# Layer 1's small sums on 32x32 tiles of TensorE, with masks stored twice and loaded per step

## The chip, the core and the metric

The kernel runs on one core of one Trainium2 chip. The metric is the device time of one execution in microseconds (us); lower is better. Engines are named as in the profile: PE (TensorE matmuls), PEld (TensorE weight loads), DVE (VectorE), ACT (ScalarE), POOL (GpSimd) and SP (SyncE, which here only issues DMAs).

## What is computed

Two layers on 4096 nodes with 512 features and a dense 4096x4096 matrix `adj`, 1 to 2% of whose elements are not zero. Layer 0 is attention with `adj` added twice to the logits; layer 1 is graph attention with 8 heads of 64 dimensions:

```python
h = relu(layernorm(x));  q, k, v = h @ Wq.T + bq, h @ Wk.T + bk, h @ Wv.T + bv
x = x + softmax(q @ k.T / sqrt(512) + adj + adj) @ v
h = relu(layernorm(x))
nX = standardize((h @ W) per head) * a_ln + b_ln          # 8 heads x 64
kg = leaky_relu(at1[:, :, None] + at2[:, None, :], 0.2) * adj   # at1 = nX.a1, at2 = nX.a2
attention = softmax(where(adj != 0, kg, -32768))
x = x + elu(attention @ nX + nX)
```

## The kernel before

**Layer 0** walks over 256 tiles of 128 sources by 512 targets (`TILES`), two tiles an iteration, with the products of the logits and of the weighted sum regrouped into seven smaller ones. Beside that work `for_layer_1` (L708) makes from each turned tile of `adj` what layer 1 needs: `ng`, bf16, is -2^60 where there is no edge and 0 elsewhere; `gs`, float32, is the edge's weight, and 2^-45 where there is none. Both go to DRAM (`nT_d`, `gT_d`) in DMAs of 128 KB and 256 KB that SP issues.

**Between the layers** the rows are normalized and projected (`turn`, `project`, `standardize`), and `sides` and `fours` put small tensors into DRAM: `z1_d` and `z2_d` hold for each head six bf16 rows (three bf16 parts of a logit's half, and ones), 32 partitions apart, so that a product over 6 rows gives a logit's sum in nearly float32; `u4_d` holds four times the targets' part.

**Layer 1** is a list of 512 steps, `STEPS`: 8 chunks of 512 targets, in each 2 groups of 4 heads (`hg`), in each 32 blocks of 128 sources. A step makes a 128x512 tile of logits for four heads (sources on the partitions, targets along the row). Two of the heads are "left", two "right":

- `left_sums` (L1070), one step ahead: the plain sums of the two left heads into a PSUM tile `l` of two banks. Four matmuls on 64x64 tiles of TensorE; the targets' operand is `z1_left`, a copy of `z1` in which everything but the six rows of the left heads is zero. `left_relu` (L1080): ACT takes four times the positive part, in place.
- `sums` (L1083): four matmuls over 6 rows add all four heads' sums (into `l` for left heads, into the banks `r0`, `r1` for right ones), then eight matmuls on 64x64 tiles add the mask, with the identity as weights. A 64-row tile of TensorE can write either half of the sources from its own 64 rows only, so the mask is held twice in SBUF: `nb`, as it is, and `nx`, with its two halves of 64 rows swapped.
- `right_leaky` (L1105): DVE makes the two right heads' logits, which frees `r0` and `r1`. `right_weigh` (L1117): POOL multiplies them by the edges' weights `g`. `left_weigh` (L1121): DVE does so for the left heads, reading `l`.
- `exponent` (L1124): ACT, two steps later, one instruction for four heads. `values` (L1128): four steps later, four float32 matmuls (eight instructions in the profile) into `accs`, which stays over the 32 steps of a group.
- `finish` (L1177) at a group's end: ACT copies one bank of `accs` and DVE the other, then PE turns the result back to rows, and the group's output is made over the next 21 steps, with three adding DMAs issued by POOL and one store issued by SP. The exponent of that step is cut in two, with the copies in between.

**Order and loads.** `seq` keeps every instruction of the steps in the order of the program, so each engine and SP's queue work in the order of the loop at L1536. `load_adj` (L1006) runs each fourth step, for the four steps after the next boundary: `z2` (128 KB), `nb` (512 KB, 128 partitions), `nx` (two DMAs of 256 KB, 64 partitions each) and `g` (1 MB, 128 partitions). Each has two buffers. `open_group` (L1033) brings `z1` and the twelve rows of `z1_left` ten steps ahead of a group, `load_u4` the targets' part.

Of the kernel before, what the change touches and what calls it, by code (L numbers as in the profile page):

```python
# [11 lines left out]
BF16 = mybir.dt.bfloat16  # L12
# [6 lines left out]
P = 128  # L19
N = 4096  # L20
D = 512
NH = 8
HD = 64
NB = N // P
SB = 4
# [10 lines left out]
GC = 512  # L36
NI = N // GC
# [42 lines left out]
def fast_path(  # L80
# [18 lines left out]
    nc = tc.nc  # L99
    seq = tc.keep_in_program_order  # L100
# [3 lines left out]
    R = 32  # L104
# [10 lines left out]
    dram = ctx.enter_context(tc.tile_pool(name="dram", bufs=1, space=DRAM))  # L115
# [29 lines left out]
    x1_d = dram.tile([NI, 2, P, SB, 2, P], F32, name="x1_d")  # L145

    gT_d = dram.tile([NB, P, N], F32, name="gT_d")
    nT_d = dram.tile([NB, P, N], BF16, name="nT_d")

# [174 lines left out]
    with tc.tile_pool(name="rows_in", bufs=2) as rows_in, tc.tile_pool(  # L326
# [357 lines left out]
        with tc.tile_pool(name="turns", bufs=6) as turns, tc.tile_pool(  # L684
# [23 lines left out]
            def for_layer_1(s):  # L708
                ic, jt = TILES[s]
                aT = turned[s] if s >= SB else firsts[s]  # L710
                ng = work.tile([P, GC], BF16, name="ng", tag="ng", bufs=2)
                seq(nc.vector.tensor_scalar(ng, aT, 0.0, NEG_BIG, ALU.is_equal, ALU.mult))
                gs = work.tile([P, GC], F32, name="gs", tag="gs", bufs=2)
                seq(nc.vector.scalar_tensor_tensor(gs, ng, G_MASKED / NEG_BIG, aT, ALU.mult, ALU.add))  # L714
                nc.sync.dma_start(out=nT_d[jt, :, ts(ic, GC)], in_=ng)
                nc.sync.dma_start(out=gT_d[jt, :, ts(ic, GC)], in_=gs)

            def product(out, s, name_a, name_b, start):
# [269 lines left out]
    with tc.tile_pool(name="ga_g", bufs=2) as adjs, tc.tile_pool(  # L988
# [5 lines left out]
        JB = 4  # L994
# [4 lines left out]

        later = {}  # L1000

        z1_lefts = [gat.tile([P, GC], BF16, name=f"z1_left{k}") for k in range(2)]
        for z in z1_lefts:
            seq(nc.vector.memset(z, 0.0))

        def load_adj(q):  # L1006
            ic, _, jt = STEPS[q * JB]
            z2 = inputs.tile([P, JB * P], BF16, name="z2", tag="z2", bufs=2)
            seq(nc.sync.dma_start(
                out=z2, in_=z2_d[:, STEPS[q * JB][1], jt * P : (jt + JB) * P]  # L1010
            ))
            ng = inputs.tile([P, JB, GC], BF16, name="nb", tag="nb", bufs=2)
            seq(nc.sync.dma_start(
                out=ng, in_=nT_d[jt : jt + JB, :, ts(ic, GC)].rearrange("t p i -> p t i")
            ))

            nx = inputs.tile([P, JB, GC], BF16, name="nx", tag="nx", bufs=2)
            for r in range(2):
                seq(nc.sync.dma_start(
                    out=nx[ts(r, HD)],  # L1020
                    in_=nT_d[jt : jt + JB, ts(1 - r, HD), ts(ic, GC)].rearrange("t p i -> p t i"),
                ))
            g = adjs.tile([P, JB, GC], F32, name="g", tag="g", bufs=2)
            seq(nc.sync.dma_start(
                out=g, in_=gT_d[jt : jt + JB, :, ts(ic, GC)].rearrange("t p i -> p t i")
            ))
            loads[q] = (g, (ng, nx), z2)

        def cols(ic, hg):
            rows = slice(ic * GC, (ic + 1) * GC)  # L1030
# [2 lines left out]
        def open_group(n, queue):  # L1033

            ic, hg, _ = STEPS[n]
            z1_left = z1_lefts[(2 * ic + hg) % 2]
            for first in (0, HD):
                rows = slice(first, first + 6)
                seq(queue.dma_start(out=z1_left[rows, :], in_=z1_d[rows, hg, ts(ic, GC)]))
            z1 = inputs.tile([P, GC], BF16, name="z1", tag="z1", bufs=2)  # L1040
            seq(queue.dma_start(out=z1, in_=z1_d[:, hg, ts(ic, GC)]))
            u4 = inputs.tile([P, 2, GC], F32, name="u4", tag="u4", bufs=2)
            groups[ic, hg] = {"z1": z1, "z1_left": z1_left, "u4": u4}
            load_u4(n, 0, queue)

        def load_u4(n, e, queue):
# [11 lines left out]

        lefts, rights = {}, {}

        def z_product(n, hh, out, start):

            ic, hg, jt = STEPS[n]
            rows = slice(32 * hh, 32 * hh + 6)
            seq(nc.tensor.matmul(  # L1065
                out, loads[n // JB][2][rows, ts(jt % JB, P)], groups[ic, hg]["z1"][rows, :],
                start=bool(start), stop=False, skip_group_check=not start,
            ))

        def left_sums(n):  # L1070

            lefts[n] = psum.tile([P, 2, GC], F32, name="l", tag="l", bufs=2)
            ic, hg, jt = STEPS[n]
            for r, c in ((0, 0), (1, 1), (0, 1), (1, 0)):
                seq(nc.tensor.matmul(  # L1075
                    lefts[n][ts(c, HD), r, :], loads[n // JB][2][ts(r, HD), jt % JB * P + c * HD :][:, :HD],
                    groups[ic, hg]["z1_left"][ts(r, HD), :], start=True, stop=True,
                ))

        def left_relu(n):  # L1080
            seq(nc.scalar.activation(lefts[n], lefts[n], AF.Relu, scale=4.0))  # L1081

        def sums(n):  # L1083

            jt = STEPS[n][2]
            left = lefts[n]
            right = [psum.tile([P, GC], F32, name=f"r{e}", tag=f"r{e}", bufs=1) for e in range(2)]
            out = [left[:, 0, :], right[0], left[:, 1, :], right[1]]
            for hh in (1, 3, 0, 2):
                z_product(n, hh, out[hh], hh % 2)  # L1090
            masks = loads[n // JB][1]
            for first in (1, 0):
                for r, c in ((0, 0), (1, 1), (0, 1), (1, 0)):
                    rows = ts(r, HD)
                    seq(nc.tensor.matmul(  # L1095
                        out[first + 2 * r][ts(c, HD), :], ident_b[rows, rows],
                        masks[r != c][rows, jt % JB, :], start=False, stop=True,
                        skip_group_check=first == 0,
                    ))
            rights[n] = right  # L1100

        def both_heads(n):
            return loads[n // JB][0][:, STEPS[n][2] % JB, :].unsqueeze(1).to_broadcast([P, 2, GC])

        def right_leaky(n):  # L1105

# [17 lines left out]
        def exponent(n, heads=slice(0, HG)):  # L1124
            t = logits[n][:, heads, :]
            seq(nc.scalar.activation(t, t, AF.Exp))  # L1126
# [337 lines left out]
        def at_block(r, f, *a):  # L1464
            at_blocks.setdefault(r, []).append(lambda: f(*a))
# [26 lines left out]
        at_block(0, rests[0])  # L1492
        at_block(12, first_group)
        at_block(14, load_adj, 0)
        for ic in range(2):
            load_normalized(ic)
        for r in range(-1, NB):
# [38 lines left out]
        for n in range(n_steps + 4):  # L1536

            q = n // JB + 1
            if n == n_steps:

                check_early()
                last_in.append(work.tile([P, HG, GC], F32, name="t", tag="t", bufs=6))
                for k, ap in enumerate((own_d[NI - 1, :, :, 1], x1_d[NI - 1, 1])):
                    seq(nc.sync.dma_start(
                        out=last_in[0][:, 2 * k : 2 * k + 2, :].rearrange("p f c -> p (f c)")
                        .rearrange("p (b d) -> p b d", b=SB),
                        in_=ap.rearrange("p b f d -> p b (f d)"),
                    ))
            if n % JB == 0 and q < n_steps // JB:
                load_adj(q)  # L1550
            if n + 10 < n_steps and STEPS[n + 10][2] == 0:
                open_group(n + 10, nc.sync)
            if n + 6 < n_steps and STEPS[n + 6][2] == 0:
                load_u4(n + 6, 1, nc.sync)
            if n < n_steps:
                sums(n)
            for f in left.pop(n, []):
                f()
            if n + 1 < n_steps:
                left_sums(n + 1)  # L1560
            if n < n_steps:
                right_leaky(n)
                right_weigh(n)
            if n + 1 < n_steps:
                left_relu(n + 1)
            done, ready = 0 <= n - 4 < n_steps, 0 <= n - 2 < n_steps
            if done and n < n_steps + 1:
                values(n - 4, 0)
            extra(n, "mid")
            if n < n_steps:  # L1570
                left_weigh(n)
            if done:
                if n < n_steps + 1:
                    values(n - 4, 1)
                if n % JB == 3:
                    loads.pop((n - 4) // JB)
            if n == n_steps + 3:
                for m, hf in ((n - 6, 0), (n - 5, 0), (n - 6, 1), (n - 5, 1)):
                    values(m, hf)
                for hf in range(2):  # L1580
                    values(n - 4, hf)
            if done and STEPS[n - 4][2] == NB - 1:
                if ready:
                    exponent(n - 2, slice(0, 2))
                finish(n, *STEPS[n - 4][:2])
                if ready:
                    exponent(n - 2, slice(2, 4))
            elif ready:
                exponent(n - 2)
            extra(n, "end")  # L1590
# [404 lines left out]
```

## Time and profile before

| | |
|---|---|
| time, median of 3 runs (3539.04 to 3541.75) | 3539.05 us |
| the profiled execution: its time, its span | 3538.39 us, 3536.6 us |
| PE busy | 3492.0 us (99%) |
| DVE busy | 2574.3 us (73%) |
| POOL busy | 2285.6 us (65%) |
| ACT busy | 1771.1 us (50%) |
| moved by DMA | 779.07 MB, 220 GB/s on average |

All times are of one execution seen by the hardware profiler. "Span" is from the first to the last instruction. A share of busy time is a mean over stages: layer 0 with its projections takes about the first 1775 us, layer 1's steps run from about 1935 to 3514 us. "DMA share" is the time that the packets on the core's 16 DMA engines took, as a share of 16 engines' time; packets can overlap, so a stretch can read above 1. Matmul durations overlap too, since matmuls are pipelined: what a matmul occupies is read from the distance between starts, or from the chain of waits, which gives each piece only the time by which it moved the end. A group name such as "L1095 PE MATMUL r<-nb,ident_b 64*64 64x512" has the line, the engine, the operation, output and inputs, the array's rows and columns in use, and the moving operand's shape.

### The profile page before, as it was taken

Reading aid. Unit: us, or ns where it says so; the run is one execution under the profiler, and the core shown is the slowest. Engines: PE = TensorE matmul, PEld = TensorE weight load, DVE = VectorE, ACT = ScalarE, POOL = GpSimd, SP = SyncE. Lnnn points to the kernel's source line nnn. Section 1 sums busy time; section 2 is a strip of 40 time slices with the busy share of each in tenths; the row PEclk is TensorE's granted clock in tenths of the full one; section 3 lists DMA queues with packets and bytes.
Section 4 is the critical chain, followed back from the end, with each engine's and each line's share of the span. In section 5 each row is a group of like instructions: output and inputs, shape, how many; then the busy total and the mean of one; then the engine's idle time right before and its main releaser. Section 6 shows DMA issues by size and latency. Waiting matters only on the chain.

```text
span 3536.6 us, 59808 instructions
## 1 busy us (share of the span) xinstructions
PE 3492.0 (99%) x21898; PEld 2149.6 (61%) x21898; DVE 2574.3 (73%) x4262; ACT 1771.1 (50%) x1580; POOL 2285.6 (65%) x1863
## 2 busy tenths in 40 slices
PE   9999999999999999999999999999999999999998
PEld 7888888888888888888887223223222323232232
DVE  6765665656565666656567888888888888888887
ACT  2100111111111111111133999999999999999997
POOL 6754444444444444444567888788888888888886
PEclk9999999999999999999999999999999999999999
DMA  6688888888888888888768777787778877777885
GB/s 226 219 247 246 233 232 250 234 244 247 235 246 247 231 252 241 237 248 232 235 135 183 210 207 204 205 208 214 211 209 219 214 215 206 198 209 209 214 213 147
DMA packets 633550, 779.07 MB, mean 220 GB/s; under 512 B 78560, under 2 KB 461216, under 8 KB 624032
## 3 DMA queue, kind: packets, MB, share of 16 engines
q1 hardware_dynamic: 615680, 742.34, 73.5%
q0 software_dynamic: 16464, 31.98, 5.3%
q8 instruction: 174, 2.85, 0.3%
q10 hardware_dynamic: 1104, 0.85, 0.1%
q14 instruction: 128, 1.05, 0.1%
HBM read 592.97 MB, written 174.19 MB: 217 GB/s over the span
## 4 chain that ended last, share of the span: by engine, by line
PE 90%; DVE 7%; ACT 1%; DMA 1%; issue 1%; SPq 0%; DVEq 0%; ACTq 0%
PE accs L1134 25%; PE XZ L722 21%; PE M L777 20%; PE r L1095 4%; PE r L1065 4%; PE l L1075 3%; PE X L508 3%; PE l L1095 3%; PE Z L508 2%; DVE t L1122 2%; PE y L1327 1%; PE pt L1198 1%; DVE x L837 1%; DVE y L1211 1%; PE accs L1327 1%
## 5 line engine op out<-in xcount | busy, mean ns | idle before, releaser
L1119 POOL TENSOR_TENSOR t<-t,g 128x1024 f32<-128x1024 f32 x512 | 1225.6, 2406 | 268.9 <-DVE t L1113 233.3
L1134 PE MATMUL accs<-t,nX 128*64 128x512 f32 x4096 | 1003.0, 605 | 4.6 <-DVE ob L1188 4.6
L1126 ACT ACTIVATE t<-t 128x2048 f32<-128x2048 f32 (+1 forms) x527 | 976.5, 1853 | 0.2 <-POOL t L1119 0.2
L1113 DVE SCALAR_TENSOR_TENSOR t<-u,at2m,r 128x512 f32<-128x512 f32 x1024 | 719.3, 744 | 194.2 <-issue 152.0
L738 ACT ACTIVATE aT<-aT 128x512 f32<-128x512 f32 x256 | 161.2, 630 | 1387.3 <-DVE aT L734 1387.3
L734 DVE TENSOR_TENSOR aT<-aT,XZ 128x256 f32<-128x256 f32 x884 | 348.7, 418 | 575.1 <-PE XZ L722 570.8
L1122 DVE TENSOR_TENSOR t<-l,g 128x1024 f32<-128x1024 f32 x512 | 623.4, 1218 | 0.0
L1081 ACT ACTIVATE l<-l 128x1024 f32<-128x1024 f32 x512 | 516.3, 1008 | 117.5 <-PE l L1075 66.2
L1134 PEld LDWEIGHTS accs<-t,nX 128*64 128x64 f32 x4096 | 246.5, 136 | 461.9 <-issue 449.5
L722 PE MATMUL XZ<-qt,hS 128*128 128x256 f32 x2024 | 479.1, 379 | 1.0
L750 POOL TENSOR_TENSOR S<-aT 128x256 f32<-128x256 f32 x128 | 93.5, 731 | 506.9 <-ACT aT L738 506.9
L722 PEld LDWEIGHTS XZ<-qt,hS 128*128 128x128 f32 x2024 | 383.9, 190 | 55.9 <-DVE aT L734 4.0
L722 PE MATMUL XZ<-qt,hT 128*128 128x256 f32 x1520 | 369.5, 379 | 0.0
L762 POOL TENSOR_TENSOR total<-total,aT 128x256 f32<-128x256 f32 x360 | 323.0, 910 | 9.4
L722 PEld LDWEIGHTS XZ<-qt,hT 128*128 128x128 f32 x1520 | 288.8, 190 | 39.3
L1065 PEld LDWEIGHTS <-z 6*128 6x128 bf16 x2048 | 52.4, 91 | 422.2 <-DVE t L1113 353.8
L751 POOL TENSOR_TENSOR aT<-aT 128x256 f32<-128x256 f32 x128 | 93.6, 731 | 284.1 <-ACT aT L738 284.0
L777 PE MATMUL M<-tv,aT 128*128 128x256 f32 x1024 | 262.6, 379 | 0.0
L777 PE MATMUL M<-v,aT 128*128 128x256 f32 x1024 | 262.6, 379 | 0.0
L777 PE MATMUL M<-v,S 128*128 128x256 f32 x1024 | 242.5, 380 | 0.0
L714 DVE SCALAR_TENSOR_TENSOR gs<-ng,aT 128x512 f32<-128x512 bf16 x252 | 222.7, 884 | 8.7
L777 PEld LDWEIGHTS M<-v,aT 128*128 128x128 f32 x1024 | 194.6, 190 | 26.5
(267 smaller groups left out, 4552.4 us busy)
## 6 DMA issues: line engine op xcount, KB each, us to landing
g<-gT_d SPq DMA_DIRECT2D x128, 1024.0 KB
ag<-in_adj_dram SPq DMA_DIRECT2D x256, 256.0 KB
hS<-s_d SPq DMA_DIRECT2D x64, 1024.0 KB
gT_d<-gs SPq DMA_DIRECT2D x256, 256.0 KB
nb<-nT_d SPq DMA_DIRECT2D x128, 512.0 KB
nx<-nT_d SPq DMA_DIRECT2D x256, 256.0 KB
hT<-h_d SPq DMA_DIRECT2D x64, 768.0 KB
tv<-vt_d SPq DMA_DIRECT2D x128, 384.0 KB
```

Source lines behind the costliest of these rows:

```text
L714: seq(nc.vector.scalar_tensor_tensor(gs, ng, G_MASKED / NEG_BIG, aT, ALU.mult, ALU.add))
L722: seq(nc.tensor.matmul(out, a, b, start=start and k == 0, stop=k == 1, skip_group_check=not start,))
L734: seq(nc.vector.tensor_add(p, before, part))
L762: seq(nc.gpsimd.tensor_add(t, t, a))
L777: seq(nc.tensor.matmul(sums[ic][i][:, u, :], a[:, ts(u, P)], b, start=jt == 0 and u == 0, stop=jt == NB - 2, skip_group_check=u == 1,))
L1081: seq(nc.scalar.activation(lefts[n], lefts[n], AF.Relu, scale=4.0))
L1095: seq(nc.tensor.matmul(out[first + 2 * r][ts(c, HD), :], ident_b[rows, rows], masks[r != c][rows, jt % JB, :], start=False, stop=True, ski ...
L1113: seq(nc.vector.scalar_tensor_tensor(t[:, 2 + e, :], u4[:, e, :], at2m[:, jt, h : h + 1], right[e], ALU.max, ALU.add))
L1119: seq(nc.gpsimd.tensor_mul(t[:, 2:4, :], t[:, 2:4, :], both_heads(n)))
L1122: seq(nc.vector.tensor_mul(logits[n][:, 0:2, :], lefts.pop(n), both_heads(n)))
L1126: seq(nc.scalar.activation(t, t, AF.Exp))
L1134: seq(nc.tensor.matmul(accs[ts(e, HD), hf, :], nX[jt // SB][:, jt % SB, hg * HG + 2 * hf + e, :], t[:, hf + 2 * e, :], start=jt == 0, stop ...
```

## The change

It puts layer 1's left sums, its 6-row sums and its mask sums on tiles of 32 rows by 32 columns: head `hh` of the step has rows 32·`hh` to 32·`hh`+31 of TensorE, and each of the four column strips writes one block of 32 sources. A matmul over 128 or 64 columns of weights becomes four or two of 32 columns: 8 matmuls a step for the left sums (before 4), 16 for all heads' sums (before 4), 16 for the masks (before 8). For this each row group needs the whole tile's mask in its own 32 partitions: 32 partitions by 4 blocks by 512 targets, four times. `for_layer_1` stores the mask twice in the new layout; `load_masks` loads a step's masks, 512 KB, in two DMAs of 64 partitions, three steps ahead, into four buffers. `nx`, `z1_left` and their loads go. The load of `g` moves from the first to the second step of each four. At a group's end the copies now come before the whole exponent, which stays one instruction.

```diff
-    nT_d = dram.tile([NB, P, N], BF16, name="nT_d")
+    nT_d = dram.tile([NB, NI, 2, R, SB, GC], BF16, name="nT_d")
...
-                nc.sync.dma_start(out=nT_d[jt, :, ts(ic, GC)], in_=ng)
+                for u in range(2):
+                    nc.sync.dma_start(out=nT_d[jt, ic, u].rearrange("p c i -> c p i"), in_=ng)
                 nc.sync.dma_start(out=gT_d[jt, :, ts(ic, GC)], in_=gs)
...
-        z1_lefts = [gat.tile([P, GC], BF16, name=f"z1_left{k}") for k in range(2)]
-        for z in z1_lefts:
-            seq(nc.vector.memset(z, 0.0))
...
         def load_adj(q):
             ic, _, jt = STEPS[q * JB]
             z2 = inputs.tile([P, JB * P], BF16, name="z2", tag="z2", bufs=2)
             seq(nc.sync.dma_start(
                 out=z2, in_=z2_d[:, STEPS[q * JB][1], jt * P : (jt + JB) * P]
             ))
-            ng = inputs.tile([P, JB, GC], BF16, name="nb", tag="nb", bufs=2)
-            seq(nc.sync.dma_start(
-                out=ng, in_=nT_d[jt : jt + JB, :, ts(ic, GC)].rearrange("t p i -> p t i")
-            ))
-
-            nx = inputs.tile([P, JB, GC], BF16, name="nx", tag="nx", bufs=2)
-            for r in range(2):
-                seq(nc.sync.dma_start(
-                    out=nx[ts(r, HD)],
-                    in_=nT_d[jt : jt + JB, ts(1 - r, HD), ts(ic, GC)].rearrange("t p i -> p t i"),
-                ))
+            loads[q] = {"z2": z2}
+
+        def load_g(q):
+            ic, _, jt = STEPS[q * JB]
             g = adjs.tile([P, JB, GC], F32, name="g", tag="g", bufs=2)
             seq(nc.sync.dma_start(
                 out=g, in_=gT_d[jt : jt + JB, :, ts(ic, GC)].rearrange("t p i -> p t i")
             ))
-            loads[q] = (g, (ng, nx), z2)
+            loads[q]["g"] = g
+
+        masks = {}
+
+        def load_masks(n):
+
+            ic, _, jt = STEPS[n]
+            masks[n] = inputs.tile([P, SB, GC], BF16, name="nb", tag="nb", bufs=4)
+            for r in range(2):
+                seq(nc.sync.dma_start(
+                    out=masks[n][ts(r, HD)], in_=nT_d[jt, ic].rearrange("u p c i -> (u p) c i")
+                ))
...
         def open_group(n, queue):
...
-            z1_left = z1_lefts[(2 * ic + hg) % 2]
-            for first in (0, HD):
-                rows = slice(first, first + 6)
-                seq(queue.dma_start(out=z1_left[rows, :], in_=z1_d[rows, hg, ts(ic, GC)]))
...
-        def z_product(n, hh, out, start):
+        def z_products(n, hh, out, **flags):
 
             ic, hg, jt = STEPS[n]
-            rows = slice(32 * hh, 32 * hh + 6)
-            seq(nc.tensor.matmul(
-                out, loads[n // JB][2][rows, ts(jt % JB, P)], groups[ic, hg]["z1"][rows, :],
-                start=bool(start), stop=False, skip_group_check=not start,
-            ))
+            rows = slice(R * hh, R * hh + 6)
+            for c in range(SB):
+                seq(nc.tensor.matmul(
+                    out[ts(c, R), :], loads[n // JB]["z2"][rows, jt % JB * P + c * R :][:, :R],
+                    groups[ic, hg]["z1"][rows, :], **flags,
+                ))
 
         def left_sums(n):
 
             lefts[n] = psum.tile([P, 2, GC], F32, name="l", tag="l", bufs=2)
-            ic, hg, jt = STEPS[n]
-            for r, c in ((0, 0), (1, 1), (0, 1), (1, 0)):
-                seq(nc.tensor.matmul(
-                    lefts[n][ts(c, HD), r, :], loads[n // JB][2][ts(r, HD), jt % JB * P + c * HD :][:, :HD],
-                    groups[ic, hg]["z1_left"][ts(r, HD), :], start=True, stop=True,
-                ))
+            for r in range(2):
+                z_products(n, 2 * r, lefts[n][:, r, :], start=True, stop=True)
...
         def sums(n):
...
-            for hh in (1, 3, 0, 2):
-                z_product(n, hh, out[hh], hh % 2)
-            masks = loads[n // JB][1]
-            for first in (1, 0):
-                for r, c in ((0, 0), (1, 1), (0, 1), (1, 0)):
-                    rows = ts(r, HD)
+            order = (1, 3, 0, 2)
+            for hh in order:
+                right_one = hh % 2 == 1
+                z_products(n, hh, out[hh], start=right_one, stop=False, skip_group_check=not right_one)
+            for hh in order:
+                rows = ts(hh, R)
+                for c in range(SB):
                     seq(nc.tensor.matmul(
-                        out[first + 2 * r][ts(c, HD), :], ident_b[rows, rows],
-                        masks[r != c][rows, jt % JB, :], start=False, stop=True,
-                        skip_group_check=first == 0,
+                        out[hh][ts(c, R), :], ident_b[rows, rows], masks[n][rows, c, :],
+                        start=False, stop=True, skip_group_check=hh % 2 == 0,
                     ))
+            masks.pop(n)
...
         at_block(14, load_adj, 0)
+        at_block(14, load_g, 0)
+        for n in range(3):
+            at_block(14, load_masks, n)
...
-            if n % JB == 0 and q < n_steps // JB:
-                load_adj(q)
+            if n + 3 < n_steps:
+                load_masks(n + 3)
+            if n % JB < 2 and q < n_steps // JB:
+                (load_adj, load_g)[n % JB](q)
...
             if done and STEPS[n - 4][2] == NB - 1:
-                if ready:
-                    exponent(n - 2, slice(0, 2))
                 finish(n, *STEPS[n - 4][:2])
                 if ready:
-                    exponent(n - 2, slice(2, 4))
+                    exponent(n - 2)
```

## The prediction

> **What bounds the kernel now.** I read the page first, then the chain of waits in a steady stretch of layer 1, the instructions in order of time there, and the busy times of short windows for the DMA engines.
>
> ```profile
> PE 3492.0 (99%) x21898; PEld 2149.6 (61%) x21898; DVE 2574.3 (73%) x4262; ACT 1771.1 (50%) x1580; POOL 2285.6 (65%) x1863
> ...
> ACT  2100111111111111111133999999999999999997
> ...
> DMA  6688888888888888888768777787778877777885
> ```
>
> PE is busy throughout; ACT is idle in layer 0 and nearly full in layer 1, and the DMA engines are three quarters full in both. The change is in layer 1, whose chain repeats with a period of 2.97 us:
>
> ```profile
> 2600.09 1.87 PE accs L1134 x8
> 2601.96 0.32 PE r L1065 x2
> 2602.28 0.01 PE l L1065 x2
> 2602.29 0.34 PE r L1095 x4
> 2602.63 0.22 PE l L1095 x4
> 2602.85 0.22 PE l L1075 x4
> ```
>
> All of it is PE: the values 1.87, the four heads' sums 0.33, the masks 0.34 + 0.22, the left sums 0.22. But the timeline has another engine right behind:
>
> ```profile
> 2602.22 0.14 PEld L1095 LDWEIGHTS <-ident_b 64*64 64x64 bf16 x8 [0.23 <-issue]
> 2602.22 0.40 PE L1095 MATMUL r<-nb,ident_b 64*64 64x512 bf16 x2
> 2602.23 0.40 PE L1095 MATMUL r<-nx,ident_b 64*64 64x512 bf16 x2
> ...
> 2603.11 1.01 ACT L1081 ACTIVATE l<-l 128x1024 f32<-128x1024 f32 x1
> ...
> 2604.03 1.91 ACT L1126 ACTIVATE t<-t 128x2048 f32<-128x2048 f32 x1
> ```
>
> ACT needs 1.01 + 1.90 = 2.91 us a step (its exponent reads 1.90 or 1.91). No PE saving can be worth more than 2.97 - 2.91 = 0.06 us a step. DVE needs 2 x 0.74 + 1.22 = 2.71 and POOL 2.41 by the page's means. That leaves the DMA engines, and here the windows matter (columns: stretch and length, busy times by engine, granted clock, DMA share, GB/s):
>
> ```profile
> 1939.00:3520.00 1581.00, 1564.01 (x12761) 468.29 (x12763) 1343.85 (x1687) 1461.98 (x1072) 1292.14 (x602) 1.00 0.78 208
> ...
> 2628.50:2629.00 0.50, 0.50 (x10) 0.18 (x12) 0.50 (x1) 0.50 (x1) 0.50 (x1) 1.00 1.06 350
> ...
> 2630.50:2632.50 2.00, 2.00 (x22) 0.51 (x18) 1.60 (x3) 2.00 (x2) 1.37 (x1) 1.00 1.02 199
> ...
> 2633.50:2634.50 1.00, 1.00 (x6) 0.14 (x2) 1.00 (x2) 1.00 (x2) 0.49 (x2) 1.00 1.04 393
> ...
> 1779.00:1785.00 6.00, 6.00 (x30) 5.28 (x29) 1.77 (x5) 0.63 (x1) 0.72 (x1) 1.00 1.05 241
> ```
>
> The first is all of layer 1's steps. The next three follow one call of `load_adj`, its DMAs in the order of the queue: `nb` over 128 partitions at 350 GB/s, `nx` in two pieces of 64 partitions at 199, `g` over 128 at 393. `nb` and `nx` have the same 1 KB runs, so the loss is the pieces', not the runs'. The last is between the layers, where SP had twelve loads of `xn_d` queued, each over 32 partitions: 241 GB/s with the engines full. Loads that cover part of the partitions move about half.
>
> **The change part by part.** *TensorE.* The eight mask matmuls, two passes of the array, become sixteen on sixteen different tiles, one pass: the second one's 0.22 us goes. Sums, masks and left sums now have one tile shape; the sums' 0.32 and the first mask pass's 0.34 stand 0.10 to 0.12 above a bare pass of 0.22, a gap at each change of shape, and the one between them goes, about 0.10. So 2.97 - 0.22 - 0.10 = 2.65 us. Added are 24 pairs of weight load and matmul a step. No row shows a 32x32 pair. The eight loads of L1095 take 0.14 us together, 18 ns each: 24 x 18 = 0.43, and a step of 3.08, if none is hidden; four such matmuls start within 0.01 us of each other, some 3 ns apart: 24 x 3 = 0.07, and 2.72. I take 2.72, since the loads overlap matmuls in the trace; both ends stay for the range. The Trainium skill speaks against this part: its page "TensorE: Matmul & The Clock Gate" (section "Wait — 56ns, not 53.3ns?") says that with hardware decoding off the sequencer spends about 62 ns on each matmul. By that, an estimate, 48 matmuls a step would take 2.98 us and nothing would be gained; no row of this trace shows which decoding holds.
>
> *Masks in layer 1.* The bytes double, from 256 to 512 KB a step, and all now come in pieces of 64 partitions, with 4 KB runs. Take a group of 32 steps: 1581 / 16 = 98.8 us, of which the DMA engines are busy 0.78 x 98.8 = 77.1; full stretches read 1.04, so 77.1 / 1.04 = 74.1 us of full work. Out go `nb`, 8 x 524,288 B at 350 GB/s = 12.0, and `nx`, 8 x 524,288 B at 199 = 21.1. What stays (`g`, `z2`, `u4`, the groups' ends) is 41.0 us. In come 32 x 524,288 B. At 393 GB/s, as if halves cost nothing, 42.7; at 199, as `nx`, 84.3; at 241, as the loads of `xn_d`, 69.6 us (2.18 a step). I take 241: there the queue was never empty, as here, and runs were 2 KB, nearer to 4 than `nx`'s 1. The sum is 110.6 us a group, against 98.8 now and 32 x 2.91 = 93.1 of ACT plus the groups' ends: the DMA engines become the bound, at 3.46 us a step. Since they then work without a break, the 98.8 - 32 x 2.97 = 3.8 us that a group's end costs now are inside the 110.6. Cost: 16 x (110.6 - 98.8) = +189 us.
>
> The Trainium skill bears on this row: its page "SBUF — State Buffer" (section "Door 1: The DMA port swizzle (why `[64,N]` ≈ `[32,N]`)") holds that 64 adjoining partitions reach only eight of the sixteen ports, and its section "Can I just issue two DMAs to hit both halves?" that two loads on the two halves gain only 6%. Its 218 GB/s for eight ports, with 6% on top, would be 231 GB/s: by it, an estimate, 72.6 us of masks a group and +237 us.
>
> *The new wait.* The first mask matmul of a step waits for its own load, before for one of four steps ago. Queued behind it on PE are the left sums of the next step and the values; DVE (`right_leaky`), ACT (`left_relu`) and POOL wait for these in turn. On SP, `load_masks` waits until `sums` of the step before has freed its buffer, with `z2`, `g`, `u4` and the output's store behind it; as three steps' masks are then still queued at the engines, they do not run dry. `g` is queued right behind the masks of the step that first uses it and takes 1,048,576 B / 393 GB/s = 2.7 us: POOL and DVE get it late once in four steps, in a gap that the sum already holds. SP itself issues an `nx` piece in 1.39 / 2 = 0.7 us (L1019), so two a step are 1.4 of 3.46 us, with room.
>
> *Layer 0.* 256 more stores of 128 KB. At the 350 GB/s of a 1 KB load that is 0.37 us of DMA each, 256 x 0.37 = 96 us in all, beside PE, whose chain there waited 0.8 us for a DMA in the whole layer; the engines' share goes from 0.83 to about 0.89. On SP each takes 0.32 us and stands ahead of the `gT_d` store and, at times, of `adj` and hidden-state loads; SP waits 824 us there for DVE, so it has the time. I take zero; if the cover is gone, up to 96 us; a gain is excluded, as nothing leaves.
>
> *The rest.* 32 loads of 6 KB and two memsets go: nothing. The copies move ahead of half an exponent, 1.05 us, of which PE waits 0.31 us at a group's end; ACT's copies and halves 2 x 1.05 become one of 1.90. At most 0.5 us x 15, hidden once DMA bounds: zero here.
>
> Sum, on the profiled execution: span 3536.6 + 189 = 3725.6, and 1.8 us outside the span: 3727. The median of the runs stands 0.7 above the profiled one: **3728 us**.
>
> **The rivals.** *ACT becomes the bound (faster).* If the two pieces overlap so that the masks come at over (32 x 524,288 B) / (98.8 - 41.0 us) = 290 GB/s, the DMA work fits into today's period. Then a step is 2.91 us, a group 32 x 0.06 + 0.4 = 2.3 us shorter, the whole 3539 - 37 = 3502 us. For it: shares of 1.05 show packets in flight together, and 4 KB runs pay less per packet. Against it: both rows of partial loads stay at 199 and 241. Chance 0.11.
>
> *The pieces run as `nx` does (slower still).* At 199 GB/s a group is 125.3 us: +26.5 x 16 = +424, 3963 us. PE's pauses could lengthen it: after its stall of 3.56 us at 1941 the granted clock fell (0.91 over 1900 to 2000 us), and mask matmuls took 0.64 instead of 0.40 us. For it: same pieces, same halves; against: `nx` had 1 KB runs and a queue that emptied after it. Chance 0.17 for 3850 and above.
>
> *TensorE doesn't gain and the masks nearly fit.* At 3.08 us a step from unhidden loads, with masks above 290 GB/s, 0.11 x 512 = +56: 3595 us. Chance 0.10 for 3530 to 3640.
>
> **How the numbers follow.** The forecast (DMA bound, 3640 to 3850) has 0.62. The range of 3580 to 3940 leaves out ACT's case (0.11), half of the last rival and the top of the second: about 0.2. Anything within 0.2% (7 us), which is what measurements of this kernel can resolve, needs the masks to hit the break-even closely: 0.02. Faster 0.11, slower 0.87.
>
> **What would show it.** Right: layer 1's DMA share near 1.04 and some 260 GB/s (208 x 98.8 us + 8.4 MB, over 110.6 us); PE waiting at the mask line for a DMA into `nb`; ACT's share of layer 1 down from 92% to about 83%; step distances of 3.46 us on average, uneven by fours; layer 0's slices unchanged; on PE three passes of about 0.22 us in one tile shape. Wrong: DMA share below 0.95 in layer 1, waits for "issue" on PE at the mask or sum lines, a period of 2.91 us with ACT unbroken, or a layer 0 that is longer.

## The result, and the profile after

The changed kernel takes **4118.22 us** (median of 4 runs, 4108.91 to 4134.45), the kernel before 3539.05; the ratio is 1.164, with a 95% interval of 1.162 to 1.166. The direction was forecast, the size was not: 3728 us with a range up to 3940. The profiled execution of the changed kernel took 4121.95 us, its span 4120.1.

The page first, in the rows that were shown of before:

```profile
PE 3643.6 (88%) x34186; PEld 2201.6 (53%) x34186; DVE 2554.1 (62%) x4260; ACT 1767.8 (43%) x1565; POOL 2227.7 (54%) x1863
...
ACT  2100111011111111110237777777777777787776
...
DMA  6677778788788877877689999999999999999997
```

In layer 1 the DMA row stands at 9 nearly from end to end and ACT has gone from 9 to 7: that part of the forecast is there in kind, though ACT was forecast at 83% and, in the window of 2500 to 3400 us below, is at 75%. But ACT's row leaves its low digits, where layer 1 begins, in about the same slice as before, although a slice is now 103 us instead of 88: layer 0 has become longer too. Layer 0 is taken here from the first start of its exponent on ACT (`aT<-aT`) to the last, layer 1 from the first start of a mask matmul to the last:

| us | before | after | difference |
|---|---|---|---|
| layer 0 (256 tiles) | 241.7 to 1785.3 = 1543.6 | 242.3 to 2027.0 = 1784.7 | +241 |
| between the layers | 151 | 154 | +3 |
| layer 1 (16 groups of 32 steps) | 1936.5 to 3511.8 = 1575.3 | 2181.3 to 4095.6 = 1914.3 | +339 |

Layer 1's loss was forecast at 189, layer 0's at zero.

**Layer 1.** The chain of waits over 2600 to 2614 us (start, length, link):

```profile
2599.85 0.27 PE l L1063 x8
2600.12 0.34 SPq L1026
2600.45 0.05 issue
2600.51 15.13 DMA nb<-nT_d
```

Before, this chain was PE from link to link. Now one link, loads of masks behind each other, fills 15 us. The instructions in order of time show the step that the forecast hoped for, and what comes of it:

```profile
2601.87 0.14 PEld L1063 LDWEIGHTS <-z 6*32 6x32 bf16 x16 [0.81 <-DVE t L1107]
...
2604.78 0.41 PE L1063 MATMUL r<-z,z 6*32 6x512 bf16 x8
...
2605.00 0.40 PE L1089 MATMUL r<-nb,ident_b 32*32 32x512 bf16 x8
...
2605.25 0.40 PE L1063 MATMUL l<-z,z 6*32 6x512 bf16 x8
...
2605.58 1.94 PE L1128 MATMUL accs<-t,nX 128*64 128x512 f32 x8
...
2607.45 0.41 PE L1063 MATMUL r<-z,z 6*32 6x512 bf16 x8
...
2612.33 0.61 PE L1089 MATMUL r<-nb,ident_b 32*32 32x512 bf16 x4 [4.45 <-DMA nb<-nT_d]
```

From 2604.78 to 2607.45 runs a whole step with its masks in place: sums 0.22, masks 0.25, left sums 0.33, values 1.87, together 2.67 us. One load of masks later, PE stands for 4.45 us.

**Layer 0.** The list of waits over 150 to 1780 us (engine, tile and line, what it waited for: us in total, times, longest) has two new rows of waits for a DMA, and one of PE's weight loads for POOL; before, PE waited 0.8 us for `tv`, once, and no weight load for POOL:

```profile
PE M L778 <- DMA tv<-vt_d: 120.6, 68, 4.4
...
PEld M L778 <- POOL aT L752: 53.0, 23, 2.6
...
DVE ng L712 <- DMA nT_d<-ng: 50.3, 19, 7.1
```

And yet the DMA engines are *less* busy there than before. The windows (stretch, its length, busy times of PE, PEld, DVE, ACT and POOL, granted clock, DMA share, GB/s), of before:

```profile
300.00:1700.00 1400.00, 1398.28 (x6497) 1228.99 (x6496) 863.06 (x1636) 182.22 (x289) 655.45 (x861) 1.00 0.84 240
```

and of after, with two short ones in which hardly anything but the new stores is under way:

```profile
300.00:1700.00 1400.00, 1263.72 (x5606) 1080.98 (x5607) 722.89 (x1411) 156.34 (x248) 526.22 (x744) 0.97 0.80 227
2500.00:3400.00 900.00, 768.94 (x11644) 231.19 (x11641) 626.38 (x778) 677.17 (x490) 595.26 (x273) 0.92 1.02 242
1006.00:1008.00 2.00, 1.04 (x3) 0.89 (x4) 0.00 (x0) 0.00 (x0) 1.84 (x4) 0.73 0.30 107
1019.00:1022.00 3.00, 3.00 (x16) 2.44 (x15) 1.81 (x3) 0.63 (x1) 0.79 (x2) 1.00 0.26 95
```

A share of 0.26 to 0.30 with a queue of stores waiting is the sign to look for: a quarter of sixteen engines, at 95 GB/s. In these windows, by the reading of the next section, four engines worked and twelve had next to nothing. The packet records of the trace, counted by time, agree: over 1019 to 1022 us four packets were under way for three quarters of the time and never more than seven; over 2603 to 2606 us, in layer 1, never fewer than sixteen. The share is a mean over sixteen, so four full engines look like slack.

### The profile page after: what moved, and what is told of

The parts are those of the page before. It is cut to its first block, busy times and chain, and to the rows that moved or that the text cites. A ratio compares the mean times of both kernels' runs of the same rounds, so it can differ in the third digit from the quotient of the medians.

```text
span 4120.1 us, 85374 instructions
## 1 busy us (share of the span) xinstructions
PE 3643.6 (88%) x34186; PEld 2201.6 (53%) x34186; DVE 2554.1 (62%) x4260; ACT 1767.8 (43%) x1565; POOL 2227.7 (54%) x1863
## 5 line engine op out<-in xcount | busy, mean ns | idle before, releaser
L1128 PE MATMUL accs<-t,nX 128*64 128x512 f32 x4096 | 1110.7, 662 | 7.6 <-DVE ob L1182 7.0
L1120 ACT ACTIVATE t<-t 128x2048 f32<-128x2048 f32 x512 | 973.2, 1901 | 10.9 <-POOL t L1113 10.7
L1128 PEld LDWEIGHTS accs<-t,nX 128*64 128x64 f32 x4096 | 263.1, 145 | 468.9 <-issue 456.2
L1063 PEld LDWEIGHTS <-z 6*32 6x32 bf16 x12288 | 169.6, 89 | 632.9 <-DVE t L1107 292.6
L1063 PE MATMUL l<-z,z 6*32 6x512 bf16 x8192 | 437.7, 403 | 44.6 <-DVE t L1116 23.2
L1089 PE MATMUL r<-nb,ident_b 32*32 32x512 bf16 x4096 | 265.0, 400 | 215.2 <-DMA nb<-nT_d 214.6
L723 PE MATMUL XZ<-qt,hT 128*128 128x256 f32 x1520 | 399.0, 402 | 0.0
L723 PEld LDWEIGHTS XZ<-qt,hT 128*128 128x128 f32 x1520 | 308.1, 203 | 47.6
L778 PE MATMUL M<-tv,S 128*128 128x256 f32 x512 | 167.8, 411 | 155.9 <-DMA tv<-vt_d 140.0
L763 POOL TENSOR_TENSOR total<-total,aT 128x256 f32<-128x256 f32 x360 | 270.5, 765 | 9.4
```

The lines of the kernel that those rows point to most:

```text
L723: seq(nc.tensor.matmul(out, a, b, start=start and k == 0, stop=k == 1, skip_group_check=not start,))
L763: seq(nc.gpsimd.tensor_add(t, t, a))
L778: seq(nc.tensor.matmul(sums[ic][i][:, u, :], a[:, ts(u, P)], b, start=jt == 0 and u == 0, stop=jt == NB - 2, skip_group_check=u == 1,))
L1063: seq(nc.tensor.matmul(out[ts(c, R), :], loads[n // JB]["z2"][rows, jt % JB * P + c * R :][:, :R], groups[ic, hg]["z1"][rows, :], **flags,))
L1089: seq(nc.tensor.matmul(out[hh][ts(c, R), :], ident_b[rows, rows], masks[n][rows, c, :], start=False, stop=True, skip_group_check=hh % 2 == ...
L1128: seq(nc.tensor.matmul(accs[ts(e, HD), hf, :], nX[jt // SB][:, jt % SB, hg * HG + 2 * hf + e, :], t[:, hf + 2 * e, :], start=jt == 0, stop ...
```

## The experiments

Two theories stood at the outset. The first: layer 0 loses because the new store, written in four blocks of 32 rows, runs on four of the sixteen DMA engines; layer 1 loses because loads over 64 partitions are slow. The rival: what costs is the number and the bytes of the new transfers (256 more stores on SP, twice the mask bytes), however they are shaped. The first runs undo the shapes one by one and leave number and bytes as they are. (Letters in the quoted expectations are defined there or name these theories in this order.) Six of the kernels take masks of other sources or of another chunk, as their expectations say, and so do not compute the whole; they serve to time the transfers. Where no number of runs is given, it is one run; the four runs of the changed kernel lie within 26 us.

**The stores as 128 rows.**

```diff
-    nc.sync.dma_start(out=nT_d[jt, ic, u].rearrange("p c i -> c p i"), in_=ng)
+    nc.sync.dma_start(out=nT_d[jt, ic, u].rearrange("p c i -> (p c) i"), in_=ng)
```

> The changed kernel, but both stores of a tile's mask go out as 128 rows of 1 KB in the order of the partitions (destination 128 x 512) and not as 4 blocks of 32 rows (destination 4 x 32 x 512). Same bytes, same number of DMAs; the masks stand in DRAM in another order of sources than the loads take them for, so that each source has another one's mask. Theory A (the stores in four blocks keep only 4 of the 16 DMA engines busy, which the share of 0.26 at 95 GB/s in stretches with nothing else suggests): layer 0, which takes 1785 us from the first to the last exponent in the changed kernel and 1544 before, goes back to about 1544, layer 1 stays at 1915, the whole is about 3877 us. Theory B (a third store a tile is too much for SP's queue, or 256 more stores are too many bytes beside layer 0's loads): layer 0 stays at about 1785, the whole at about 4118 us.

Measured: 3864.38 us; layer 0 1543.6, layer 1 1900. The window of its layer 0:

```profile
300.00:1700.00 1400.00, 1398.17 (x6497) 1228.76 (x6496) 862.82 (x1636) 182.25 (x289) 655.73 (x862) 1.00 0.92 262
```

As many stores and bytes as in the change, PE as full as before the change, and a share that rises by 0.08. So 256 stores of 128 KB cost nothing in layer 0, as the prediction had it; their shape costs 241 us.

**The mask loads over all 128 partitions**, two DMAs of 256 KB as before, each with 2 KB a partition instead of 4 KB on half of them:

```diff
+    pair = nT_d[jt, ic - ic % 2 : ic - ic % 2 + 2].rearrange("n u p c i -> (n u p) c i")
     for r in range(2):
-        out=masks[n][ts(r, HD)], in_=nT_d[jt, ic].rearrange("u p c i -> (u p) c i")
+        out=masks[n][:, 2 * r : 2 * r + 2], in_=pair[:, 2 * r : 2 * r + 2]
```

> The changed kernel, but a step's 512 KB of masks come in two DMAs over all 128 partitions, half of the columns each, and not over 64 partitions each. Same bytes, same number of DMAs. The 128 partitions are filled from two neighbouring chunks' masks, so two of the four heads get another chunk's masks. Theory A (pieces over 64 partitions run at half the rate): the masks of a group of 32 steps take 32 x 524,288 B at 393 GB/s = 42.7 us, 84 with all else, under the 96 us that ACT and the groups' ends need: layer 1 falls from 1915 us to about 1550 and the whole to about 3750 us; layer 0 stays at 1785. Theory B (twice the mask bytes are too many however they come, or at most eight DMAs in flight on SP's queue hold the loads back): layer 1 stays above 1850 us, the whole above 4050.

Measured: 3761.28 us; layer 0 1781.8, layer 1 1561. Its two windows show each layer's loss by itself:

```profile
300.00:1700.00 1400.00, 1264.60 (x5622) 1081.12 (x5623) 726.75 (x1416) 156.31 (x248) 526.20 (x747) 0.97 0.80 227
2500.00:3400.00 900.00, 856.35 (x14384) 277.69 (x14367) 769.95 (x963) 830.46 (x607) 735.99 (x341) 1.00 0.90 298
```

Layer 0's clock, share and rate are the changed kernel's to the digit. Layer 1 moves the same bytes at 298 GB/s where the change reaches 242, with a tenth of the engines' time to spare, and its loss of 339 us is gone.

**Both together.**

> Both edits together: stores as 128 rows, mask loads over 128 partitions. Masks of the wrong sources and, for two heads, of another chunk. Theory A: both losses go and only TensorE's part is left: a step is bound by ACT at 2.91 us, TensorE needs about 2.7, layer 0 takes 1544 us, layer 1 about 1545, the whole 3505 us (1% under the kernel before). If the 24 more weight loads and matmuls a step bind TensorE, layer 1 is at 1576 or more and the whole at 3540 or above. Theory B: over 3900 us.

Measured: 3526.3 us (5 runs, 3525.25 to 3529.34), ratio 0.9963 (0.9949 to 0.9977); layer 0 1544.3, layer 1 1566. The two causes add up to the whole of it. Of the 37 us that the prediction's bound by ACT allows (3539 to 3502), only 12 came, so something still stood in the way. A third theory came from here, that SP's queue, with a limited number of DMAs in flight, holds the loads back; it is tested below.

The next runs asked how the loss of layer 0 grows, and tested the steps taken at zero.

**One store a tile, in the four blocks.** `nT_d` loses its `u`, and one store is left:

```diff
-    for u in range(2):
-        nc.sync.dma_start(out=nT_d[jt, ic, u].rearrange("p c i -> c p i"), in_=ng)
+    nc.sync.dma_start(out=nT_d[jt, ic].rearrange("p c i -> c p i"), in_=ng)
```

> The changed kernel with one store of a tile's mask in four blocks instead of two; the loads over 64 partitions take the two copies from two neighbouring chunks (two heads get another chunk's masks). A dose of the suspected cost. Theory A: the four engines have per tile 0.84 x 6.1 - 0.4 = 4.7 us of other work and 128 x 1 KB at 95 GB/s = 1.4 us of stores, 6.1 us against a tile's 6.1 us of TensorE: layer 0 loses little, 0 to 60 us of the 241, and the whole is 3880 to 3940 us. Theory B (bytes, or the number of DMAs, with no threshold at the four engines): before had one store too, so all of the 241 goes and the whole is 3877 with no layer 0 loss at all; a rate loss in proportion to the stores in blocks: half of it, 3998.

Measured: 3873.33 us; layer 0 1555.5. PE's wait for `tv` over 300 to 1700 us falls from 111.1 us in the changed kernel to

```profile
PE M L777 <- DMA tv<-vt_d: 4.7, 12, 1.1
```

A loss in proportion to the block stores would have left about 120 of the 241 us; 12 are left. By itself this run does not tell theory A (0 to 60 us) from theory B (none); the first experiment does.

**The stores alone**: the kernel before, with two block stores a tile added to a tensor that nothing reads.

```diff
+    for u in range(2):
+        nc.sync.dma_start(out=more_d[jt, ic, u].rearrange("p c i -> c p i"), in_=ng)
```

> The kernel before, plus two stores of each tile's mask in four blocks of 32 rows, into a tensor that nothing reads. Theory A (four engines): per tile these have the 5.1 us of before and 256 x 1 KB at 95 GB/s = 2.8 us more, against 6.1 us of TensorE: layer 0 grows by 240 to 400 us, layer 1 stays at 1576, the whole is 3780 to 3940 us. Theory B (the loss in layer 0 of the changed kernel has to do with what its later loads need): 3539 us.

Measured: 3870.44 us; layer 0 1876, layer 1 1576, before 1575. Over 300 to 1700 us PE waits for `tv`:

```profile
PE M L780 <- DMA tv<-vt_d: 135.3, 65, 5.1
```

The three points fit one sum, an estimate from the windows. Before, a tile takes 1543.6 / 256 = 6.03 us and holds 0.84 / 1.04 x 6.03 = 4.87 us of full DMA work, spread over sixteen engines; 0.37 of it is the plain store. A block store puts 131,072 B / 95 GB/s = 1.38 us on four of them. With one block store in place of the plain one, these four have 4.87 - 0.37 + 1.38 = 5.88 us, still under 6.03 (measured 6.08). With two, 7.26 (measured 1784.7 / 256 = 6.97). With two beside the plain one, 7.63 (measured 1876 / 256 = 7.33). The last two are 4% high, but the step at the tile's length is right: the second store is the one that costs.

**The copies first, alone**: the kernel before with `finish` ahead of a whole exponent.

```diff
-    if ready: exponent(n - 2, slice(0, 2))
     finish(n, *STEPS[n - 4][:2])
-    if ready: exponent(n - 2, slice(2, 4))
+    if ready: exponent(n - 2)
```

> The kernel before, with only the order at a group's end changed: the copies of accs, then the exponent as one instruction. The prediction put this at zero where DMA bounds and at no more than 0.5 us x 15 groups elsewhere: 3531 to 3539 us, most likely 3534. Rival: the exponent that now comes after the copies reaches the values two steps later by up to 0.6 us later, with no room, and gives back what the copies gain: 3539 us or a little above.

Measured: 3539.1 us (11 runs), ratio 1.0001 (0.9992 to 1.001). Its timeline says why:

```profile
2640.63 0.58 ACT L1187 COPY ob<-accs 128x512 f32<-128x512 f32 x1 [0.85 <-PE accs L1134]
```

ACT's copy waits for PE's last values; before the change it begins at 2640.58, behind a half exponent that had filled this wait. Going first brings nothing forward. The time is that of the rival in the expectation, but not for its reason: there was no gain to give back.

**The second piece from ACT's queue**, on the first experiment's kernel, in case two pieces on two halves run side by side once they do not share a queue:

```diff
-    for r in range(2):
-        seq(nc.sync.dma_start(out=masks[n][ts(r, HD)], ...))
+    for r, queue in enumerate((nc.sync, nc.scalar)):
+        seq(queue.dma_start(out=masks[n][ts(r, HD)], ...))
```

> The first experiment's kernel (stores as 128 rows; masks of the wrong sources), with the second of a step's two mask pieces issued by ACT and not by SP, so that the two halves of the partitions can be in flight at once. ACT's issue takes about 0.4 us a step (0.41 for its output store), so a step is at least 3.3 us. Theory H1 (one queue in order keeps all engines on one half at a time, and that alone halves the rate): the masks come at 300 GB/s or more, ACT bounds, layer 1 falls from 1900 to about 1700 us and the whole to about 3660. Theory H2 (the engines' work for two halves adds up, whatever the order, which the Trainium skill's page on SBUF, section on two DMAs for both halves, says with a gain of 6%): layer 1 at 1820 to 1920, the whole 3780 to 3880 us.

Measured: 3911.1 us; layer 1 1931, against 1900 from one queue. The rate does not move (246 GB/s from one queue in the same window), and new waits come on top: ACT stands for earlier loads of masks to land, and PE for ACT.

```profile
2500.00:3400.00 900.00, 770.03 (x11716) 236.26 (x11713) 629.27 (x781) 682.49 (x495) 607.03 (x281) 0.90 1.03 244
```

```profile
PE l L1063 <- ACT l L1075: 96.2, 35, 6.4
...
ACT l L1075 <- DMA nb<-nT_d: 65.5, 20, 5.7
```

The Trainium skill's page "SBUF — State Buffer" (section "Can I just issue two DMAs to hit both halves?") says that two concurrent DMAs, one on each half, reached only 6% more than a single one; here a second queue gained nothing over one queue that holds pieces of both halves.

**A step's masks in one DMA** of 512 KB, 4 KB a partition on all 128, on the kernel with both undone:

```diff
-    for r in range(2):
-        seq(nc.sync.dma_start(out=masks[n][:, 2 * r : 2 * r + 2], in_=pair[:, 2 * r : 2 * r + 2]))
+    seq(nc.sync.dma_start(out=masks[n], in_=pair))
```

> As the third experiment (stores as 128 rows, mask loads over 128 partitions; masks of the wrong sources and, for two heads, of another chunk), but a step's masks in one DMA of 512 KB in runs of 4 KB and not in two with runs of 2 KB. The third one took 3526 us where ACT's 2.91 us a step would give 3505, with waits for masks and for g in every fourth step. Theory C (SP's queue holds at most eight DMAs in flight, of which the two pieces take more than they need): with half the mask DMAs the loads go out earlier, the waits go, 3505 to 3512 us. Theory D (the bytes themselves come late: a share of 0.91 on average leaves too little room in the steps with g): 3520 to 3530 us as before; longer runs alone are worth a few us at most.

Measured: 3490.98 us (4 runs), ratio 0.9861 (0.9846 to 0.9876); layer 1 1526.4 instead of 1566, below the numbers of both theories.

```profile
2500.00:3400.00 900.00, 859.55 (x14718) 282.57 (x14716) 787.78 (x990) 846.32 (x619) 751.70 (x345) 1.00 0.91 304
```

Against the kernel before these are -48 us, or 1526.4 / 16 = 95.4 us a group: what the change's work on TensorE was worth here, with the DMA engines no longer full. It is the rival "ACT becomes the bound", with 3502 forecast; why it came out lower is told below. The gain over two DMAs is shown, its reason is not: half as many DMAs and runs of 4 instead of 2 KB came together. For the limit on DMAs in flight speaks what SP waits for. In the changed kernel its loads of masks wait for earlier loads to land, in layer 1:

```profile
SPq L1026 <- DMA g<-gT_d: 357.1, 104, 6.7
...
SPq L1026 <- DMA nb<-nT_d: 261.7, 436, 2.5
```

With two DMAs over 128 partitions these two rows are 68.7 and 74.5 us, with masks in one DMA 18.3 and 53.7. The traces also show the limit: SP's DMAs take turns on eight semaphores, and, counted from issue to landing over 2500 to 3400 us, eight were in flight for 30% of the time with two DMAs a step and for 7% with one, never more.

The last two runs asked whether the whole change can be mended, with nothing of the computation altered.

**The two stores as four DMAs of 32 rows**, each writing both copies of its block, so that 32 is the outermost size; the loads as in the change:

```diff
-    for u in range(2):
-        nc.sync.dma_start(out=nT_d[jt, ic, u].rearrange("p c i -> c p i"), in_=ng)
+    for c in range(SB):
+        nc.sync.dma_start(
+            out=nT_d[jt, ic, :, :, c, :].rearrange("u p i -> p u i"),
+            in_=ng[ts(c, R)].unsqueeze(1).to_broadcast([R, 2, GC]),
+        )
```

> The change with its two stores a tile written as four DMAs of 32 rows, each writing both copies; the loads stay as the change has them, and nothing of the computation is left out. If only the outer dimension of 4 kept the stores on four engines, layer 0 returns to 1545 to 1560 us (DMA work of a tile 4.9 - 0.37 + 262,144 B / 241 GB/s = 5.6 us at most, under 6.05), layer 1 stays at 1900 to 1915, in all 3865 to 3880 us. If what delays layer 0 is the number of SP's stores or the blocks of 32 rows as such, layer 0 stays near 1785 and the whole near 4118.

Measured: 3879.6 us; layer 0 242.2 to 1803.1 = 1560.9, layer 1 1897.5. More stores on SP, the same bytes, and 224 of the 241 us are back:

```profile
300.00:1700.00 1400.00, 1389.46 (x6438) 1215.93 (x6437) 856.76 (x1621) 181.49 (x287) 643.56 (x848) 1.00 0.93 260
```

It is the outer size of 4, not the blocks of 32 rows. Where the remaining 17 us come from is not shown: the stores now read from 32 partitions at a time, and there are four of them instead of two. The share is 0.93 where 128 rows had 0.92.

**Four copies**, so that one load over 128 partitions finds its rows: as the last, with 4 in place of 2, and the load in one DMA.

> The masks are stored four times, so that layer 1 loads a step's masks in one DMA over all 128 partitions from their own rows; the store is four DMAs a tile, one for each block of 32 rows, each writing all four copies (32 source rows are the slowest dimension, so all 16 engines should share it). Nothing of the computation is left out. Layer 1: 1527 us, as with the masks in one DMA. Layer 0 decides. Theory A (stores read from 32 partitions go at the 241 GB/s of the xn_d loads over 32 partitions): a tile has 0.84 / 1.04 x 6.05 = 4.9 us of full DMA work now; less one store of 0.37 and plus 524,288 B / 241 GB/s = 2.18 makes 6.7 us, over the 6.05 that PE takes: +0.65 x 256 = +166 us, in all about 3655 us. Theory B (they cost what 128 rows cost, 0.37 us per 128 KB): 4.9 + 3 x 0.37 = 6.0 us, just under PE's 6.05: layer 0 at 1545 to 1580, in all 3490 to 3530 us, faster than the kernel before. If 32 rows do not spread over the 16 engines, layer 0 loses over 500 us.

Measured: 3580.61 us (4 runs, 3576.81 to 3596.96), ratio 1.0135 (1.0108 to 1.0161), between the two theories' numbers. Its windows:

```profile
300.00:1700.00 1400.00, 1356.36 (x6229) 1176.33 (x6228) 825.89 (x1566) 175.96 (x279) 606.11 (x820) 1.00 1.02 292
2500.00:3400.00 900.00, 857.07 (x14622) 281.13 (x14620) 782.53 (x984) 839.94 (x616) 747.32 (x344) 0.99 0.90 302
```

Layer 1 is 1541 us, 34 less than before. Layer 0 is 1616.1, 73 more: its DMA engines, sixteen of them now, are full. The gain of one layer is less than what the other pays for it. No version here that computes the whole beats the kernel before. Making some of the copies within layer 1, whose engines have a tenth of their time free, was not tried.

## Why the prediction was right and wrong

**TensorE's step, 2.72 us forecast: right.** 2.67 when nothing waits. The 24 further pairs are hidden: sixteen weight loads take 0.14 us together (2601.87), as eight did before. The upper bound of 3.08 falls. The 62 ns per matmul of the page "TensorE: Matmul & The Clock Gate" were not seen: the step's 48 matmuls passed in 2.67 us, where they would need 2.98, and eight steps behind each other in the one-DMA kernel (2563.28 to 2585.60) took 2.79 each. The page states them for hardware decoding off; which decoding held here no run shows.

**Masks in layer 1, +189 us forecast: right mechanism, one term too small.** A group took 1914.3 / 16 = 119.6 us instead of 110.6. With 41.0 us of other work the masks' term is 78.6 us, not 69.6: 16,777,216 B / 78.6 = 213 GB/s, not 241; with the measured share of 1.02 set against a full 1.04 it is 117.3 - 41.0 = 76.3 us, or 220 GB/s. The 41.0 agree with the one-DMA kernel: 0.91 / 1.04 x 95.4 = 83.5 us of full work, less 41.0 leaves 42.5, or 395 GB/s, near the 393 of `g`'s row. The step that failed is the choice between the rows 199 and 241. I took the one whose runs and queue were nearer; the measured value lies between. The page "SBUF — State Buffer", weighed there with 231 GB/s by an estimate, was nearer than my row and still above the measurement. Cost: 9.0 x 16 = 144 of the 150 us missing in layer 1; the other 6 are the difference between the prediction's 1581 us for the steps before and the table's 1575.3.

**Layer 0's stores, zero forecast, bound 96 us: the step that failed.** The price of a store was taken from a 1 KB load over 128 partitions, 350 GB/s on all engines, and hidden by an average share of 0.83. Both halves of that were wrong for this store and right for its bytes: as 128 rows it costs zero (first experiment), as `"p c i -> c p i"` some 1.4 us on four engines (131,072 B at 95 GB/s). The bound was no bound, because it varied only the cover and not the rate. A rule that I had not weighed says it: the Trainium skill's page "DMA: Bandwidth & Descriptors" (section "Why a DMA increments its semaphore by 16 and not by 1") has the number of engines as the largest up to 16 that divides the outermost size other than 1 of both sides. Source 128, destination 4: four engines. The trace agrees, with 0.26 of sixteen in the window at 1019 us, and so does the return of layer 0 when that size became 128 or 32. What the full engines then delayed shows in PE's wait of 120.6 us for `tv`; that such a load ends late because its part on these four does is inferred, as the trace does not name the engine of a packet.

**The copies at the groups' ends, zero: right**, 3539.1 against 3539, though not because DMA hid them; ACT had to wait for PE in either order.

**The sum mended.** 189 + 241 (layer 0) + 150 (layer 1) + 3 (between the layers) = 583, and the span rose from 3536.6 to 4120.1, by 583.5.

**The rivals.** "ACT becomes the bound" needed 290 GB/s; over 128 partitions the masks had it, in pieces of 64 they did not. Its bound of 2.91 us a step, from the prediction's first part, was none: it adds durations that overlap. In the rows shown there ACT's `l` starts at 2603.11 and takes 1.01, and the exponent starts at 2604.03. Where ACT has no pause its exponents start 2.74 us apart, as in the kernel with both shapes undone:

```profile
2598.64 1.89 ACT L1121 ACTIVATE t<-t 128x2048 f32<-128x2048 f32 x1
...
2600.44 1.00 ACT L1076 ACTIVATE l<-l 128x1024 f32<-128x1024 f32 x1
...
2601.38 1.89 ACT L1121 ACTIVATE t<-t 128x2048 f32<-128x2048 f32 x1
...
2603.18 1.00 ACT L1076 ACTIVATE l<-l 128x1024 f32<-128x1024 f32 x1
...
2604.12 1.89 ACT L1121 ACTIVATE t<-t 128x2048 f32<-128x2048 f32 x1
```

By these rows a saving on PE could be worth 2.97 - 2.74 = 0.23 us a step and not 0.06, which is how 3491 could come out below 3502. "The pieces run as `nx`" put layer 1 at +424; it came to +339. That the whole fell into this rival's band (3850 and above) is chance: 241 us of it are layer 0's. "TensorE doesn't gain" is out, with 2.67 us a step and the 48 us above. None of them looked at layer 0, and "a layer 0 that is longer" stood only among the signs of a wrong forecast. The granted clock did fall after PE's pauses, to 0.92 on average in layer 1, but with the DMA engines at a share of 1.02 it is more likely a result of the waits than a cause; no run parts the two.

## What to carry to other kernels

Before a rearranged store or load is priced by its bytes, look at the outermost size of both sides: with 4 the store ran on four engines here, with 32 or 128 the loss was gone. Where fewer engines work, the time counts on those alone, on top of all else they carry. A mean DMA share with room in it proves nothing then; add up the fullest engine, and find its sign in the trace in a stretch where only that transfer is under way (0.26 for four of sixteen). An engine's period is read from the distance between starts and not from a sum of durations (2.74 against 2.91 us on ACT). And a layout that needs the same bytes on several partition groups was paid for here by the writer, 73 us for four copies, or by the reader, 339 us where the copies did not fill all 128 partitions.

## What the runs showed of the hardware

- Two DMA shapes with the same bytes and 1 KB runs: 128 rows cost the layer nothing, 4 x 32 rows 95 GB/s and four engines. One such store a tile was hidden (+12 us in 256 tiles), two were not (+241): a threshold, not a slope.
- Loads over 64 partitions, alternating between the halves in a queue that is never empty, with 4 KB a partition: 213 to 220 GB/s by the two workings above; over 128 partitions, by the second of them, 395. Two issuing queues instead of one changed nothing for the better (layer 1 1931 against 1900 us).
- TensorE took 40 matmuls on tiles of 32 columns (16 sums, 16 masks, 8 left sums) with as many weight loads in 0.80 us of a step of 2.67 us, some 20 ns for a pair.
- ACT's two instructions of a step, of 1.00 and 1.89 us, passed every 2.74 us where it had no pause.
- SP's DMAs take turns on eight semaphores: never more than eight were in flight.
- Four copies read from 32 partitions at a time: with them layer 0 ran at 292 GB/s and a share of 1.02. By the working of the block stores, an estimate, a tile then holds 1.02 / 1.04 x 1616.1 / 256 = 6.19 us of full work; less the 4.87 - 0.37 of the rest, 1.69 us are left for 524,288 B, or 310 GB/s: dearer than rows of 128, for which the prediction had 350, cheaper than the 241 that loads over 32 partitions had suggested.
